# A routed mixture of experts inside a fused four-layer kernel: results stay in their slots and the next layer gathers and weighs them

## The chip, the cores and the metric

The kernel runs on one core of one Trainium2 chip. A core has a matmul engine (TensorE, PE), a vector engine (VectorE, DVE), an activation engine (ScalarE, ACT), a general-purpose engine (GpSimd, POOL) and a sync engine (SyncE, SP), each with its own instruction queue; they meet through semaphores. Two on-chip memories, SBUF and PSUM (where matmuls write), have 128 partitions; DRAM lies outside and is reached by DMA. POOL, SP and ACT can issue DMAs. An indirect DMA, issued by POOL, takes a list of row numbers, one per partition, and moves one row of DRAM for each: from SBUF to DRAM it scatters, the other way it gathers.

The metric is the time of one execution on the device in microseconds, as the median of several runs. The profile is of one execution of its own.

## The reference

Four layers follow one another on the same 8,192 tokens of 128 features in float32 (32 x 256 x 128 at the input, regrouped from layer to layer). Each layer is an attention-like block and a feed-forward block, with a residual addition and a normalization in front of each. Layer 0 has a state-space block and an expert-choice mixture of 16 experts. Layer 1 has a linear attention and the mixture below. Layer 2 has an attention with 16 heads of 8 features over sequences of 256 tokens and a low-rank mixture. Layer 3 has a smoothing block and a block of attention and a mixture with one expert per token.

What matters here is the feed-forward block of layer 1. Each token takes its two best of eight experts, weighed by a softmax over the two scores:

```
logits = xf @ gate_w + gate_b
top_w, top_i = jax.lax.top_k(logits, K)            # K = 2
gw = jax.nn.softmax(top_w, axis=-1)
combine = (gw[:, :, None] * one_hot(top_i, E)).sum(axis=1)
for e in range(E):                                  # E = 8
    h = gelu(xf @ w1[e] + b1[e])                    # 128 -> 512
    out = out + combine[:, e:e+1] * (h @ w2[e] + b2[e])
shared = gelu(xf @ ws1 + bs1) @ ws2 + bs2
return out + shared
```

The kernel computes only the two experts that a token has chosen.

## The kernel before

**Data.** The activations stay in SBUF for the whole kernel as `K.x`, 128 partitions x 64 blocks x 128 features; block j holds tokens 128j to 128j + 127. `NT` is 64, `P` and `D` are 128.

**Slots.** The class `Slots` holds the machinery of routing, once for layer 1 (`slots1`, tensors `f1_rows` and `f1_back`, two ranks: first and second choice) and once for layer 3 (`slots3`, `f3_rows` and `f3_back`, one rank). `rows` is a tensor in DRAM with one region of 8,448 rows per expert. A row has 130 floats (520 bytes): the token's 128 normalized features, the row of `back` to which its result belongs, and its weight. `back` holds first as many rows that nobody reads, for slots without a token, and behind them one row for each token and rank, in the order of the tokens.

**Fill.** `Slots.fill` runs in layer 0's feed-forward stage. It writes every slot of `rows` with zeros and with the slot's own number as its destination, so that an empty slot's result goes to a row that nobody reads. POOL makes the numbers (iota, L328) in one of two `blank` buffers and issues a DMA of 390 KB (L332), 88 for each of the two `Slots`.

**Sends.** In layer 1, while PE computes the shared expert (`rise` and `fall`, L1550 to L1574), coroutines advanced by `beside` normalize tokens, compute the gate and its best two, and count out a slot for each (`places`); DVE writes the slot numbers into two `slot` tiles from a pool of two buffers. Then POOL writes the destination (`belongs`, an iota, L368) and the weight (a copy, L1407) into the rows and issues, for each block and rank, one indirect DMA (`send`, L473): 128 in all, in four chunks of 16 blocks, the first rank and then the second.

**Experts.** `Slots.experts` goes through 72 groups of 256 slots (40 in layer 3). A group belongs to one expert; its first slot and its expert come from small tables and are read into registers. `fetch` loads the 256 rows (`xs`, on SP) and the weights, and PE transposes them; `rise` computes h (L533, L539); `fall` computes o (L549, L553), DVE multiplies by the weight column (`y`, L555), and POOL issues two scatters of 128 rows (`result`, L479). One step of the loop runs `rise` of one group, `fetch` of the next and `fall` of the one before.

**Entry of layer 2.** In `l2_attn` a generator `enter` works in groups of eight blocks. For each it loads `back`'s first and second rank (`results`, L574, 512 KB on SP, three buffers), adds each to `K.x` (DVE, L2022), takes the statistics of the blocks and finishes the normalization in small steps. `beside` advances it by two steps each time that the attention calls it; `rows` runs it further where the next two blocks aren't ready. POOL then makes the normalized blocks `xn` (L2039), which PE transposes (L1732) and projects (L1743). Between projection and scores the heads pass through DRAM (`d<-low`, `k<-d`, `q<-row`).

**Order.** In these stages the program's own order holds for PE, ACT and DVE, in the experts for SP too. A scheduler arranges POOL, and SP elsewhere. Each queue runs in order, so an instruction that waits holds those behind it. Writes to different rows of one DRAM tensor are declared free of each other (`free`).

## Time and profile before

| what | value |
|---|---|
| runs | 3314.72, 3316.81 (median), 3318.75 us |
| profiled execution | 3323.56 us; its span 3321.8 us |
| granted PE clock | 0.89 of full speed |
| PE busy | 2661.6 us (80%) |
| weight loads (PEld) busy | 1897.2 us (57%) |
| DVE busy | 1843.3 us (55%) |
| ACT busy | 1409.0 us (42%) |
| POOL busy | 844.5 us (25%) |
| POOL's DMAs (queue 0) | 97.92 MB, 7.7% of 16 engines' span |
| SP's and ACT's DMAs (queue 1) | 237.01 MB, 25.1% |

The stages stand one after another in the span:

| us | stage | PE busy | DVE busy | POOL busy | DMA share |
|---|---|---|---|---|---|
| 363-674 | layer 0's experts, with the fill | 255.21 of 311 | 138.06 | 123.74 | 0.60 |
| 674-859 | layer 0's experts, after the fill | 180.19 of 185 | 107.93 | 0.57 | 0.07 |
| 859-1026 | layer 1's attention and gate | 137.63 of 167 | 127.99 | 32.17 | 0.03 |
| 1026-1301 | layer 1's shared expert, routing and sends | 156.37 of 275 | 34.97 | 116.23 | 0.14 |
| 1310-1636 | layer 1's routed experts | 321.96 of 326 | 124.15 | 137.02 | 0.20 |
| 1636-1860 | layer 2's attention, with its entry | 167.32 of 224 | 157.73 | 28.58 | 0.52 |
| 1860-2240 | layer 2's attention | 341.20 of 380 | 266.19 | 30.55 | 0.43 |
| 2400-3104 | layer 3's attention, with its sends | 539.11 of 704 | 505.92 | 186.06 | 0.38 |
| 3104-3247 | layer 3's routed experts | 114.82 of 143 | 57.48 | 76.52 | 0.26 |

How to read it: the shares of the whole span are averages over stages with different limits, so a change is judged in its stage. A row of the groups gives line, engine, operation, written and read tiles, shape and count; then busy time and the mean of one in ns; then the engine's idle time just before these instructions and what ended it. The chain of waits goes back from the last instruction, at each step to what released it; a piece has its start, its length and its name. "issue" is time in which the engine waited for nothing that the profile shows, and "remote" or "another core or an unknown queue" stands where no instruction in the profile accounts for the release. A DMA on POOL is shown while POOL works on the issue; the transfer itself is apart.

### The profile page before, as it was taken

The numbers are of one execution on the slowest core, as the hardware profiler recorded it, in microseconds if no ns is written. First come the engines' busy times: TensorE is split into PE (matmuls) and PEld (weight loads), VectorE is DVE, ScalarE is ACT, GpSimd is POOL, SyncE is SP. The second block draws the span as 40 slices with busy tenths as digits, with TensorE's granted clock in tenths as the row PEclk, the third lists the DMA queues.
The fourth block names the chain that finished last, engine by engine and source line by source line (L and its number), as shares of the span: only waits on it lengthen the run. The fifth ranks groups of instructions, "written<-read, shape, count | busy, mean of one in ns | idle before, by whom it ended". The sixth has DMA issues, their size and how long they took to land.

```text
span 3321.8 us, 59216 instructions
## 1 busy us (share of the span) xinstructions
PE 2661.6 (80%) x21597; PEld 1897.2 (57%) x21598; DVE 1843.3 (55%) x5368; ACT 1409.0 (42%) x2988; POOL 844.5 (25%) x1227
## 2 busy tenths in 40 slices
PE   5999778999795457999778998988988888786580
PEld 4765444446564335888656777757655555554460
DVE  6115445436874111333368877755788877774446
ACT  3323432223463222333425555557246655553123
POOL 0001444300015341444310010001501332323463
PEclk9899889999898778999869999997979988997795
DMA  2377455620002010122165444420054444440223
GB/s 67 110 247 238 177 233 228 232 73 6 11 1 88 26 35 15 60 62 61 55 180 152 131 138 141 131 64 1 8 147 119 116 115 115 122 115 13 83 80 107
DMA packets 263262, 340.80 MB, mean 103 GB/s; under 512 B 34598, under 2 KB 231062, under 8 KB 254780
## 3 DMA queue, kind: packets, MB, share of 16 engines
q1 hardware_dynamic: 231228, 237.01, 25.1%
q0 software_dynamic: 27584, 97.92, 7.7%
q8 instruction: 171, 2.80, 0.4%
q10 hardware_dynamic: 4160, 2.10, 0.2%
q14 instruction: 119, 0.97, 0.1%
HBM read 156.72 MB, written 177.83 MB: 101 GB/s over the span
## 4 chain that ended last, share of the span: by engine, by line
PE 36%; DVE 16%; issue 5%; another core or an unknown queue 5%; ACT 4%; DMA 3%; POOL 2%; SPq 1%; DVEq 0%; POOLq 0%; ACTq 0%
DVE top L1803 6%; PE hp L533 5%; PE o L549 5%; PE t L1849 4%; PE o L1870 4%; PE s L1791 2%; DMA q<-row 2%; PE o L1568 2%; POOL f_back L479 1%; ACT e L1857 1%; DVE st_x L241 1%; PE hp L1554 1%; PE m L1743 1%; PE m L1908 1%
## 5 line engine op out<-in xcount | busy, mean ns | idle before, releaser
L1803 DVE TENSOR_REDUCE top<-s 128x3 f32<-128x384 f32 (+1 forms) x1024 | 598.6, 616 | 212.9 <-PE s L1702 111.2
L1857 ACT ACTIVATE e<-t 128x384 f32<-128x384 f32 (+1 forms) x1024 | 493.7, 546 | 140.0 <-PE s L1702 76.6
L1849 PE MATMUL t<-q,k 64*128 64x256 f32 (+1 forms) x2048 | 422.9, 313 | 103.0 <-ACT e L1857 77.9
L1791 PE MATMUL s<-k,q 48*128 48x256 f32 (+1 forms) x2048 | 446.5, 333 | 12.7 <-DVE top L1803 10.1
L1849 PEld LDWEIGHTS t<-q,k 64*128 64x128 f32 x2048 | 303.4, 195 | 185.4 <-ACT e L1857 108.9
L1791 PEld LDWEIGHTS s<-k,q 48*128 48x128 f32 x2048 | 312.9, 201 | 27.4 <-DVE top L1803 20.0
L479 POOL DMA_INDIRECT f_back<-y,place x224 | 216.3, 965 | 313.1 <-DVE y L555 171.8
L539 ACT ACTIVATE h<-hp,w 128x256 f32<-128x256 f32 x368 | 154.6, 471 | 328.6 <-PE hp L533 287.2
L1870 PE MATMUL o<-e,val 128*32 128x256 f32 (+1 forms) x4096 | 270.2, 385 | 0.0
L549 PE MATMUL o<-w,h 128*128 128x128 f32 x1472 | 214.3, 284 | 0.0
L533 PE MATMUL hp<-xT,w 128*128 128x256 f32 x736 | 195.2, 405 | 21.2 <-DVE xT L524 15.6
L549 PEld LDWEIGHTS o<-w,h 128*128 128x128 f32 x1472 | 183.5, 193 | 7.7
L2039 POOL TENSOR_SCALAR xn<-x_sb,mean_x,r_x 128x128 f32<-128x128 f32 x64 | 53.0, 836 | 441.7 <-PE m L1732 387.2
L1870 PEld LDWEIGHTS o<-e,val 128*32 128x32 f32 x4096 | 112.0, 114 | 91.9 <-issue 38.8
L533 PEld LDWEIGHTS hp<-xT,w 128*128 128x128 f32 x736 | 134.2, 195 | 46.2 <-DVE xT L524 20.2
L1554 PE MATMUL hp<-xnT,shared 128*128 128x512 f32 x128 | 74.2, 709 | 103.4 <-ACT h L1558 93.2
L1702 PE MATMUL s<-hideq,pick 64*128 64x128 bf16 x1024 | 151.5, 231 | 0.0
L473 POOL DMA_INDIRECT f_rows<-row,slot x128 | 122.9, 960 | 110.3 <-ACT h L1558 66.9
L1702 PE MATMUL t<-hidek,pick 64*128 64x128 bf16 x1024 | 146.2, 226 | 0.0
L555 DVE TENSOR_TENSOR y<-o,xs 128x256 f32<-128x256 f32 x112 | 47.4, 424 | 164.4 <-PE o L553 149.2
L766 PE MATMUL up<-wc,hT 128*128 128x128 f32 x768 | 129.2, 309 | 0.0
L1574 DVE TENSOR_TENSOR x_sb<-x_sb,o 128x512 f32<-128x512 f32 x16 | 11.0, 687 | 209.9 <-remote 98.9
(515 smaller groups left out, 5392.8 us busy)
## 6 DMA issues: line engine op xcount, KB each, us to landing
f_rows<-blank POOLq DMA_DIRECT2D x176, 390.0 KB
tz<-kpad SPq DMA_DIRECT2D x64, 512.0 KB
d<-high SPq DMA_DIRECT2D x128, 256.0 KB
d<-low SPq DMA_DIRECT2D x128, 256.0 KB
q<-d SPq DMA_DIRECT2D x128, 256.0 KB
k<-d SPq DMA_DIRECT2D x128, 256.0 KB
xs<-f_rows SPq DMA_DIRECT2D x112, 130.0 KB
t<-f_back SPq DMA_DIRECT2D x24, 512.0 KB
```

The source lines that it names most:

```text
L473: i = self.K.nc.gpsimd.indirect_dma_start(self.rows, bass.IndirectOffsetOnAxis(ap=slot, axis=0), row, None)
L479: i = self.K.nc.gpsimd.indirect_dma_start(self.back, bass.IndirectOffsetOnAxis(ap=place, axis=0), row, None)
L533: nc.tensor.matmul(hp[:, i, :], w[:, (c + i) * P : (c + i + 1) * P], xT, start=True, stop=True,)
L539: nc.scalar.activation(h[:, c + i, :], hp[:, i, :], act, bias=w[:, b1 : b1 + 1])
L549: nc.tensor.matmul(o[:, i, :], h[:, c, i * P : (i + 1) * P], w[:, F + c * D : F + c * D + D], start=c == 0, stop=False,)
L766: nc.tensor.matmul(o, hT[:, 2 * blk + b, s : s + P], wc[:, j, cs], start=j == 0, stop=False)
L1702: nc.tensor.matmul(t.rearrange("p (n q) -> p n q", n=3)[:, 0:3:2, 64 * n : 64 * n + 64], pick[r, n, :], hide[name][r], start=False, stop=n ...
L1791: nc.tensor.matmul(s[:, lo:hi], q[r, p, h * P : (h + 1) * P], k[r, p, 0 : hi - lo], start=h == 0, stop=not causal and h == 1,)
L1803: nc.vector.tensor_reduce(tops[b][:, :, j, p], out_of["s"][:, 0:used].rearrange("q (h k) -> q h k", h=3 if causal else 2), axis=AX.X, op=A ...
L1849: nc.tensor.matmul(t[:, kh * SEQ : kh * SEQ + SEQ - skip], k[r, p, kh * P : (kh + 1) * P], q[r, p, skip:SEQ], start=kh == 0, stop=not caus ...
L1857: nc.scalar.activation(e, t, AF.Exp)
L1870: nc.tensor.matmul(o[32 * i : 32 * i + 32, skip:SEQ], val[b % RING][:, kh, 4 * m + i, 16 * s : 16 * s + 32], e[:, kh * SEQ : kh * SEQ + SE ...
```

## The change

Only layer 1's routing and what lies around it changes; layer 3 keeps its rows of 130 floats and its scatters.

- **Rows.** `slots1` has rows of 128 floats (512 bytes): tokens alone. `belongs` and the weight copy are gone for layer 1. Slot numbers and weights are written into tiles that live until layer 2 has used them (`K.slot_of`, `K.weight_of`).
- **Results.** `y` is a plain copy of `o`, and a group's 256 results go back with one DMA on SP (`put`) into the same slots of `f1_back`. The place copy is gone for layer 1.
- **Token loads.** In both layers the load of a group's tokens is issued a step earlier in the loop: `tokens(g + 2)` at its head. In layer 1 the register with the slot's number is read once for the load and once for the store.
- **Entry of layer 2.** For each block and rank, POOL gathers the token's result from its slot (`get`, an indirect DMA into one of 24 buffers), and DVE multiplies it by the weight and adds it to `K.x` in one instruction (`scalar_tensor_tensor`). Statistics are taken by single blocks.
- **Fill.** `slots3` is filled as before. Both `f1_rows` and `f1_back` are now filled with zeros from one `blank` buffer, by 88 DMAs of 384 KB each, whose source is one row repeated six times in each partition.

```diff
@@ -305,18 +305,22 @@
 
 
 
-    GROUP, WIDE, NE = 256, D + 2, 8
+
+    GROUP, NE = 256, 8
     ROOM = NT * P + GROUP
 
-    def __init__(self, K, es, tag, ranks):
-        self.K, self.tag, self.ranks = K, tag, ranks
+    def __init__(self, K, es, tag, ranks, bring):
+        self.K, self.tag, self.ranks, self.bring = K, tag, ranks, bring
+        self.WIDE = D + 2 if bring else D
         self.groups = ranks * NT * P // self.GROUP + self.NE
         self.count = self.NE * self.ROOM
         dram = K.pool(es, tag + "slots", 1, DRAM)
         self.rows = dram.tile([self.count, self.WIDE], F32, name=f"{tag}_rows")
-        self.back = dram.tile([self.count + ranks * NT * P, D], F32, name=f"{tag}_back")
-
-    def fill(self, pool):
+        most = self.count + (ranks * NT * P if bring else 0)
+        self.back = dram.tile([most, D], F32, name=f"{tag}_back")
+
+    def fill(self, pool, other):
+
         nc = self.K.nc
         n = 6
         blank = [pool.tile([P, n, self.WIDE], F32, name=f"blank{i}") for i in range(2)]
@@ -330,6 +334,10 @@
                 allow_small_or_imprecise_dtypes=True,
             )
             nc.gpsimd.dma_start(rows[i], t)
+        for t in (other.rows, other.back):
+            rows = t.rearrange("(c p n) w -> c p n w", p=P, n=n)
+            for i in range(self.count // P // n):
+                nc.gpsimd.dma_start(rows[i], blank[0][:, 0:1, 0:D].to_broadcast([P, n, D]))
 
     def begin(self, pool, most):
 
@@ -463,6 +471,19 @@
         nc.vector.scalar_tensor_tensor(mine, mine, float(G), which, ALU.mult, ALU.add)
         nc.vector.tensor_scalar_min(start, mine, float(self.count - G))
 
+    def put(self, at, y):
+
+        i = self.K.nc.sync.dma_start(
+            self.back[bass.ds(at, self.GROUP)].rearrange("(n p) d -> p n d", p=P), y
+        )
+        self.free(self.tag + "put", i.ins)
+
+    def get(self, out, slot):
+
+        self.K.nc.gpsimd.indirect_dma_start(
+            out, None, self.back, bass.IndirectOffsetOnAxis(ap=slot, axis=0)
+        )
+
     def free(self, key, ins):
 
         self.K.tc.declare_no_dep(ins, group=key, reason="rows that differ")
@@ -497,17 +518,22 @@
             pt = K.pool(ps, tag + "gt", 2, PSUM)
             ph = K.pool(ps, tag + "gh", 4, PSUM)
             po = K.pool(ps, tag + "go", 2, PSUM)
-            state = {}
+            state, tokens_of = {}, {}
+
+            def where(g):
+                return nc.sync.value_load(
+                    start[0:1, g : g + 1], min_val=0, max_val=self.count - self.GROUP
+                )
+
+            def tokens(g):
+                xs = tokens_of[g] = gp.tile([P, N, self.WIDE], F32, name="xs")
+                nc.sync.dma_start(
+                    xs, self.rows[bass.ds(where(g), self.GROUP)].rearrange("(n p) w -> p n w", p=P)
+                )
 
             def fetch(g):
 
-                at = nc.sync.value_load(
-                    start[0:1, g : g + 1], min_val=0, max_val=self.count - self.GROUP
-                )
-                xs = gp.tile([P, N, self.WIDE], F32, name="xs")
-                nc.sync.dma_start(
-                    xs, self.rows[bass.ds(at, self.GROUP)].rearrange("(n p) w -> p n w", p=P)
-                )
+                xs = tokens_of.pop(g)
                 at = nc.vector.value_load(
                     expert[0:1, g : g + 1], min_val=0, max_val=(self.NE - 1) * LONG
                 )
@@ -515,8 +541,10 @@
                 nc.vector.tensor_copy(w, flat[:, bass.ds(at, REST)])
                 b2 = gp.tile([3, D], BF16, name="b2")
                 nc.vector.tensor_copy(b2, flat[0:3, REST:][:, bass.ds(at, D)])
-                place = gp.tile([P, N], mybir.dt.uint32, name="place")
-                nc.vector.tensor_copy(place, xs[:, :, D])
+                place = None
+                if self.bring:
+                    place = gp.tile([P, N], mybir.dt.uint32, name="place")
+                    nc.vector.tensor_copy(place, xs[:, :, D])
                 t = pt.tile([P, N * P], F32, name="t")
                 for i in range(N):
                     nc.tensor.transpose(t[:, i * P : (i + 1) * P], xs[:, i, 0:D], K.ident)
@@ -552,6 +580,10 @@
                         )
                     nc.tensor.matmul(o[:, i, :], self.every[0:3, :], b2, start=False, stop=True)
                 y = gp.tile([P, N, D], F32, name="y")
+                if not self.bring:
+                    nc.vector.tensor_copy(y, o)
+                    self.put(where(g), y)
+                    return
                 nc.vector.tensor_mul(y, o, xs[:, :, D + 1 : D + 2].to_broadcast([P, N, D]))
                 for i in range(N):
                     self.result(place[:, i : i + 1], y[:, i, :])
@@ -559,7 +591,10 @@
             with K.tc.manual_schedule(
                 engines={nc.tensor.engine, nc.scalar.engine, nc.vector.engine, nc.sync.engine}
             ):
+                tokens(0)
                 for g in range(-1, self.groups + 1):
+                    if g + 2 < self.groups:
+                        tokens(g + 2)
                     if 0 <= g < self.groups:
                         rise(g)
                     if g + 1 < self.groups:
@@ -950,8 +985,7 @@
             pos, pattern=[[1, SEQ]], base=0, channel_multiplier=0,
             allow_small_or_imprecise_dtypes=True,
         )
-        for slots in (K.slots1, K.slots3):
-            slots.fill(sp)
+        K.slots3.fill(sp, K.slots1)
         xs = sp.tile([P, 4, NB, 4, CAP], F32, name="xs")
         ew = K.pool(es, "f0e", 3)
 
@@ -1264,7 +1298,6 @@
         sp = K.pool(es, "l1", 1)
         xnT = sp.tile([P, NBLK, 512], F32, name="xnT")
         row = sp.tile([P, NT, S.WIDE], F32, name="row")
-        weight = sp.tile([P, NT], F32, name="weight")
         nmr = sp.tile([P, NT], F32, name="nmr")
         expert = sp.tile([1, S.groups], mybir.dt.int32, name="expert")
         start = sp.tile([1, S.groups], mybir.dt.int32, name="start")
@@ -1391,20 +1424,17 @@
             nc.vector.tensor_sub(e, tops[1], tops[0])
             nc.scalar.activation(e, e, AF.Exp)
             yield
-            slots = [lw.tile([P, n], mybir.dt.uint32, name=f"slot{i}") for i in range(2)]
+            slots = [t[:, lo:hi] for t in K.slot_of]
             yield from S.places(rw, lambda: hold.pop(lo), picks, slots)
             sum_e = new("sum_e")
             nc.vector.tensor_scalar_add(sum_e, e, 1.0)
             yield
-            w0 = row[:, lo:hi, D + 1]
+            w0, w1 = (t[:, lo:hi] for t in K.weight_of)
             nc.vector.reciprocal(w0, sum_e)
             yield
-            nc.vector.tensor_mul(weight[:, lo:hi], w0, e)
+            nc.vector.tensor_mul(w1, w0, e)
             yield
             for i in range(2):
-                S.belongs(row, lo, n, i)
-                if i == 1:
-                    nc.gpsimd.tensor_copy(w0, weight[:, lo:hi])
                 for j in range(lo, hi):
                     S.send(slots[i][:, j - lo : j - lo + 1], row[:, j, :])
             yield
@@ -2011,18 +2041,24 @@
 
 
         norm, after = K.norms
-        rp = K.pool(es, "a2r", 3)
+        rp = K.pool(es, "a2r", 24)
         closing = []
         ready = [0]
 
         def enter():
             for lo in range(0, NT, 8):
-                xb = K.x[:, lo : lo + 8, :]
-                for n in range(2):
-                    nc.vector.tensor_add(xb, xb, K.slots1.results(rp, n, lo))
-                    yield
-                for j in range(lo, lo + 8, 2):
-                    norm.take(K.x, j, j + 2)
+                got = {}
+                for j in range(lo, lo + 8):
+                    for n in range(2):
+                        got[j, n] = rp.tile([P, D], F32, name="t")
+                        K.slots1.get(got[j, n], K.slot_of[n][:, j : j + 1])
+                for j in range(lo, lo + 8):
+                    for n in range(2):
+                        nc.vector.scalar_tensor_tensor(
+                            K.x[:, j, :], got[j, n], K.weight_of[n][:, j : j + 1], K.x[:, j, :],
+                            ALU.mult, ALU.add,
+                        )
+                    norm.take(K.x, j, j + 1)
                     yield
                 for _ in norm.steps(lo, lo + 8):
                     yield
@@ -2621,10 +2657,17 @@
     with ExitStack() as es:
         K = Ctx(tc, ins, es)
         K.out = out
-        K.slots1 = Slots(K, es, "f1", 2)
-        K.slots3 = Slots(K, es, "f3", 1)
-        for stage in (l0_attn, l0_ffn, layer1, l2_attn):
+        K.slots1 = Slots(K, es, "f1", 2, False)
+        K.slots3 = Slots(K, es, "f3", 1, True)
+        for stage in (l0_attn, l0_ffn):
             stage(K)
+        with ExitStack() as two:
+
+            tp = K.pool(two, "two", 1)
+            K.slot_of = [tp.tile([P, NT], mybir.dt.uint32, name=f"slot_of{i}") for i in range(2)]
+            K.weight_of = [tp.tile([P, NT], F32, name=f"weight_of{i}") for i in range(2)]
+            layer1(K)
+            l2_attn(K)
         last = l3_ffn(K)
         middle(K, *next(last))
         for _ in last:
```

More of the change, by code (lines that the diff above doesn't have):

```diff
@@ L499, in experts, with fetch @@
             po = K.pool(ps, tag + "go", 2, PSUM)
-            state = {}
-            def fetch(g):
-                at = nc.sync.value_load(
+            state, tokens_of = {}, {}
+            def where(g):
+                return nc.sync.value_load(
                     start[0:1, g : g + 1], min_val=0, max_val=self.count - self.GROUP
                 )
-                xs = gp.tile([P, N, self.WIDE], F32, name="xs")
+            def tokens(g):
+                xs = tokens_of[g] = gp.tile([P, N, self.WIDE], F32, name="xs")
                 nc.sync.dma_start(
-                    xs, self.rows[bass.ds(at, self.GROUP)].rearrange("(n p) w -> p n w", p=P)
+                    xs, self.rows[bass.ds(where(g), self.GROUP)].rearrange("(n p) w -> p n w", p=P)
                 )
+            def fetch(g):
+                xs = tokens_of.pop(g)
                 at = nc.vector.value_load(
```

## The prediction

> **What bounds the kernel now.** I read the page first, then its chain of waits in the stretches that the change touches, then busy times per stretch, then groups of instructions.
>
> ```profile
> L479 POOL DMA_INDIRECT f_back<-y,place x224 | 216.3, 965 | 313.1 <-DVE y L555 171.8
> L2039 POOL TENSOR_SCALAR xn<-x_sb,mean_x,r_x 128x128 f32<-128x128 f32 x64 | 53.0, 836 | 441.7 <-PE m L1732 387.2
> L473 POOL DMA_INDIRECT f_rows<-row,slot x128 | 122.9, 960 | 110.3 <-ACT h L1558 66.9
> L1574 DVE TENSOR_TENSOR x_sb<-x_sb,o 128x512 f32<-128x512 f32 x16 | 11.0, 687 | 209.9 <-remote 98.9
> ```
>
> These four rows of the page concern us. An indirect DMA takes POOL about 0.96 us, and two starts in a series lie 1.26 us apart. The last row is odd: a DVE addition waits 98.9 us for something "remote" in a program of one core. The chain of waits for layer 1's routing (1010 to 1310 us) shows where:
>
> ```profile
> 1026.04 5.19 another core or an unknown queue
> 1031.28 7.17 another core or an unknown queue x2
> ...
> 1058.68 50.40 another core or an unknown queue
> ...
> 1155.52 19.92 another core or an unknown queue
> 1176.05 9.98 another core or an unknown queue
> ...
> 1219.42 17.52 another core or an unknown queue
> ...
> 1240.45 17.85 another core or an unknown queue
> ```
>
> That is 128 us of a stage of 275 us. The POOL sends to `f1_rows` run at 1014.8-1035, 1041-1103, 1144.8-1187 and 1212.7-1255, and each hole lies inside or at the end of such a series. Busy time over the second series:
>
> ```profile
> 1041.00:1063.00 22.00, 13.53 (x55) 8.60 (x54) 5.45 (x35) 8.83 (x15) 16.42 (x18) 0.70 0.48 144
> 1064.00:1087.00 23.00, 6.37 (x13) 2.65 (x12) 0.00 (x0) 0.00 (x0) 16.11 (x19) 0.58 0.15 49
> 1087.00:1109.00 22.00, 0.77 (x1) 0.00 (x0) 0.00 (x0) 0.00 (x0) 12.94 (x14) 0.50 0.13 42
> ```
>
> Columns: stretch, length, then busy time and count of PE, weight loads, DVE, ACT, POOL; clock, DMA share, GB/s. While POOL issues one indirect DMA after another, PE falls to 13 matmuls in 23 us and DVE and ACT to none; they wake at 1109.0, though PE's last matmul started at 1086.6. So PE's signals arrive late, with the DMA engines only 15% busy. I call this the freeze. Layer 3's series of 8 sends (10 us) show it too:
>
> ```profile
> 2780.37 5.95 another core or an unknown queue
> ...
> 2860.54 4.83 another core or an unknown queue
> ```
>
> From these: a series of n sends freezes about 1.26n - 5 us. The scatters of layer 1's experts, two per 4.44 us, show no such piece.
>
> The third place is the entry to layer 2:
>
> ```profile
> 1643.37 27.07 issue
> 1670.44 1.62 POOL xn L2039
> ```
>
> PE has nothing until the first normalized rows (`xn`) at 1670.4.
>
> **What the skill says.** The Trainium skill, "GPSIMD Engine Reference", section "When to use GPSIMD", says a pair of POOL's cores generates the descriptors of such a DMA, one the read and one the write side. "DMA: Bandwidth & Descriptors", section "Terms", puts those descriptors in rings in SBUF. Neither speaks of a freeze; if its cause is this generation, a gather must behave like a scatter. The same page's "Specifications" asks for 512 bytes per transfer for full rate; the 520-byte rows are above it, and the trace shows only a small gain to be had: packets of 4,160 B (eight rows) take 193 ns, those of 4,096 B 158 ns. "Perfetto Trace Analysis", section on SWDGE, says the shown end of such an instruction is the end of generation, not of the transfer; the trace agrees, packets follow it.
>
> **The change, part by part.** The sum is against the profiled execution, 3323.56 us (span 3321.8); the runs' median is 6.8 us lower, and I carry the difference over to it.
>
> *Sends (layer 1).* Still 128 at 1.26 us = 161 us. Gone are eight iotas, four weight copies and their waits: POOL waits 4.6 + 1.7 + 1.65 + 1.64 us between half-series plus about 0.8 us each, 13 us in all. DVE's slot casts lose their wait for a buffer. As the freeze ends with the series, most comes off the path: -10 (0 to -13).
>
> *Experts.* The stage 1310-1636 has PE busy 321.96 of 326 us. 144 scatters leave POOL, 72 stores of 128 KB go to SP behind `y`; the token loads stand two groups ahead of them in SP's queue. A 0.15 us copy per group leaves DVE (busy 124 of 326). PE's cover hides all: 0. Without it, the 72 copies would be worth 11 us.
>
> *Fill.* 176 DMAs of 390 KB become 88 of 390 KB and 176 of 384 KB, 104 MB in place of 70. Before:
>
> ```profile
> L332 POOL DMA_DIRECT2D f_rows<-blank x176 | 98.1, 557 | 54.4 <-POOL blank L328 51.5 <-issue 3.0
> ```
>
> The new ones have 768 pieces of 512 B each. Price of that: not shown; POOL's 16-piece DMAs at the start take 490-535 ns and the 128-piece ones 557, so about 0.56 ns a piece and an estimate of 0.93 us for 768; at worst proportional, 3.3 us. At the 226 GB/s of before the fill lasts 461 us, 363.6 to 825; the first send is at 1014.8 and POOL does nothing between 674 and 859. Hidden: 0. At 3.3 us it ends near 990, POOL's constants for layer 1 (at 859 now) come that late, and it costs about 130.
>
> *Entry of layer 2.* Out go 16 loads of 512 KB (on SP, the second one behind the fills of q and k until 1659.4) and 16 additions of 1.217 us (19.5 us). In come 128 gathers of 128 rows, priced by the sends: 161 us on POOL, and 128 weigh-and-add instructions on DVE; the like form at L1518 takes 343 ns alone, about 0.28 in a row: 36 us. DVE gains 17 us, in a stretch (1636-1860) where it is busy 158 of 224: 3 on the path (0 to 17). In the order that the changed program is built in, POOL has 32 gathers ahead of the first `xn`. The last store lands about 1644 (the last expert output at 1639, the store of 128 KB some 3 us, a guess between 2 and 5); 32 x 1.26 = 40, so `xn` comes at 1684.5, not 1670.4: +14 (5 to 20).
>
> *Freeze by the gathers.* The other 96 come in series of 2, 8, 14, 14, 2, 16, 8, 8, 16 and 8, with two `xn` between (0.8 us each). By the rule: 0, 5, 12.6, 12.6, 0, 15, 5, 5, 15, 5 = 75 us, in an attention with PE at 90% and a signal between engines at every step, so it is exposed. But 24 buffers pace them: DVE frees two per 2 us, and a frozen DVE frees none, which breaks a series off. I take 55; bounds 0 (gathers don't freeze) and 96 x 1.26 = 121 (no gap at all helps).
>
> Sum: -10 + 0 + 0 + 3 + 14 + 55 = +62; 3316.8 + 62 = 3379.
>
> **Rivals.** *Gathers don't freeze.* Nothing in the trace is a gather; the freeze may belong to writes into DRAM. Then -10 + 3 + 14 = +7, 3324, and with xn on time and the copies gained -14, 3303. *The freeze is due to rows of 520 bytes* and falls away with 512: then 128 us come off layer 1's stage, which is bounded by its 161 us of sends instead: they end at about 1190, the stage near 1200 in place of 1301: -100, plus 3 at the entry: about 3215. This ends on the other side; it decides if series of 512-byte rows run without late signals. Against it: layer 3's scatters into `f3_back` have 512-byte rows, and after four to six in a row (3144.6-3152.3) a transpose that ended at 3150.7 woke DVE at 3153.3, 2.6 us late. *The fill freezes or blocks layer 0's experts.* POOL would be busy generating about half the time, up to 825. Before, at 0.56 of 1.77 us, nothing froze. If PE loses a tenth of 460 us: +46 on the sum, about 3425; if generation is proportional, 3510. *Nothing moves* would need gathers hidden entirely and no gain, part of the first rival.
>
> **How the numbers follow.** Freezing gathers 0.44 (all slower; own range 3340 to 3430). Gathers without freeze 0.30 (3300 to 3340: faster 0.17, same 0.06, slower 0.07). No freeze at all 0.14 (faster). Fill 0.12 (slower). Faster 0.31, same 0.06, slower 0.63; 0.2% is 6.6 us, about what a measurement can tell from no change. Range 3225 to 3455: it takes in the first two cases, the milder third of the no-freeze case and the milder fill; outside are about 0.10 below and 0.08 above.
>
> **What would show it.** Right: in the chain of waits of 1690-1900, pieces of "another core or an unknown queue" of 5 to 15 us beside runs of gathers, some 40 to 70 us in sum; the first `xn` about 14 us later after the last expert matmul than the 32 us of before; the routing stage shorter by about 10 us with its holes still there; experts at 4.44 us a group. Wrong: holes gone from the routing stage (512-byte rows), gathers with PE at its old pace, or layer 0's experts ending later than 859. My forecast falls first if the freeze belongs to DRAM writes.

## The result, and the profile after

The changed kernel took 3410.08 us (median of 4 runs, 3409.13 to 3415.03), the kernel before 3316.04 (3314.72 to 3318.75): a ratio of 1.0285, 95% interval 1.0268 to 1.0301, so 94 us slower. The forecast was 3379, in a range of 3225 to 3455, with 0.63 for slower. The profiled execution's span went from 3321.8 to 3413.3 us, 91.5 more.

One thing has to be known for all that follows: the freeze beside series of sends was there in the measurement above and in experiments 9 to 12 (kernel before at 3316 to 3324 us), and absent in experiments 1 to 8 (3137 to 3147 us), on one chip in both ways at different times; every ratio is to the kernel before in the same group of runs.

In the profiles without the freeze no engine waits for "remote" anywhere. Stage times are of single profiles, and the same code varies in them: layer 2's attention of the kernel before took 555.2 and 558.1 us in two profiles without the freeze, and 559.5 and 565.4 in two with it. A difference under some 6 us in that stage says nothing.

The lost time by stage, from the start and end of the same PE instructions in both profiles:

| up to | before, us | after, us | shift | added here |
|---|---|---|---|---|
| last `o` of layer 0's experts | 861.3 | 862.9 | +1.6 | +1.6 |
| last `o` of layer 1's shared expert | 1301.6 | 1311.2 | +9.6 | +8.0 |
| end of layer 1's experts (the last product that prepares layer 2's weights) | 1643.4 | 1653.0 | +9.6 | 0 |
| first transposition of `xn` in layer 2 | 1672.1 | 1693.9 | +21.8 | +12.2 |
| last output projection of layer 2 | 2231.6 | 2325.5 | +93.9 | +72.1 |
| end of the span | 3321.8 | 3413.3 | +91.5 | -2.4 |

From the page of the changed kernel, the groups of sends, gathers, normalized rows (`xn`), and the addition of the shared expert:

```profile
L494 POOL DMA_INDIRECT f_rows<-row,slot_of x128 | 122.9, 960 | 120.8 <-ACT h L1588 67.0
L483 POOL DMA_INDIRECT t<-f_back,slot_of x128 | 122.9, 960 | 82.0 <-DVE x_sb L2057 36.2
L2075 POOL TENSOR_SCALAR xn<-x_sb,mean_x,r_x 128x128 f32<-128x128 f32 x64 | 50.6, 797 | 335.5 <-PE m L1762 320.4
L1604 DVE TENSOR_TENSOR x_sb<-x_sb,o 128x512 f32<-128x512 f32 x16 | 11.0, 687 | 191.6 <-PE o L1598 92.0
```

A gather costs POOL exactly what a send does, 960 ns, as the prediction had priced it. The last row no longer names "remote" first, but the holes in the routing stage are still there, now with rows of 512 bytes. Two stretches of it, in the columns that the prediction explains:

```profile
1087.00:1109.00 22.00, 0.00 (x0) 0.00 (x0) 0.69 (x1) 4.41 (x12) 16.70 (x18) 0.57 0.16 53
1226.00:1260.00 34.00, 3.99 (x19) 2.21 (x17) 0.69 (x1) 0.00 (x0) 22.98 (x24) 0.61 0.14 48
```

The changed kernel's chain of waits in layer 2's first 300 us has the start as one piece, and then holes that were not there before:

```profile
1652.97 40.96 issue
...
1725.97 3.65 another core or an unknown queue
1730.36 3.47 another core or an unknown queue
...
1799.80 3.67 another core or an unknown queue
...
1838.63 5.21 another core or an unknown queue
...
1888.62 5.11 another core or an unknown queue
...
1922.03 8.05 another core or an unknown queue
```

The longer series of gathers ran at 1653-1693 (32), 1700-1710 (8), 1714-1731 (14), 1750-1765 (12), 1789-1812 (16), 1833-1855 (16), 1877-1892 (12) and 1918-1928 (8): each hole lies in or behind such a series, and the attention stops losing time against the kernel before after about 1980. All eight such holes up to 1990 make 33 us, in pieces of 1.7 to 8 us; the prediction had looked for 40 to 70 us in pieces of 5 to 15. The waits in 1693 to 1960 say who was kept waiting:

```profile
DVE top L1833 <- remote: 41.6, 11, 5.2
ACT e L1887 <- remote: 32.9, 7, 6.6
```

The columns are the total in us, the number of waits and the longest. Both engines wait for PE's products of scores, and both for a release that no instruction accounts for. The kernel before has no such row there.

Busy time over the part of layer 2's attention with the same 2154 matmuls, before and then after:

```profile
1672.00:1881.00 209.00, 181.41 (x2154) 137.16 (x2154) 164.02 (x531) 94.13 (x221) 24.75 (x30) 0.84 0.55 156
```

```profile
1694.00:1980.00 286.00, 213.06 (x2154) 155.22 (x2154) 187.63 (x619) 94.41 (x221) 115.57 (x125) 0.71 0.41 116
```

DVE has 23.6 us more work. The matmuls themselves take 32 us more, at a granted clock of 0.71 in place of 0.84: PE is made to wait and had a lower clock as well.

### The profile page after: what moved, and what is told of

It reads as the page before. It is cut to its first block, busy times and chain, and to the rows that moved or that the text cites. A ratio compares the mean times of both kernels' runs of the same rounds, so it can differ in the third digit from the quotient of the medians.

```text
span 3413.3 us, 59764 instructions
## 1 busy us (share of the span) xinstructions
PE 2701.8 (79%) x21598; PEld 1922.6 (56%) x21598; DVE 1866.6 (55%) x5408; ACT 1409.2 (41%) x2988; POOL 902.7 (26%) x1197
## 3 DMA queue, kind: packets, MB, share of 16 engines
q0 software_dynamic: 39744, 130.80, 12.2%
## 4 chain that ended last, share of the span: by engine, by line
PE 36%; DVE 16%; issue 8%; another core or an unknown queue 4%; ACT 3%; POOL 3%; DMA 2%; SPq 1%; DVEq 0%; POOLq 0%; ACTq 0%
DVE top L1833 7%; PE hp L561 4%; PE o L577 4%; PE t L1879 4%; PE o L1900 4%; POOL f_back L500 2%; PE s L1821 2%; PE o L1598 2%; PE hp L1584 1%; ACT e L1887 1%; DVE st_x L241 1%; PE m L1773 1%; DMA q<-row 1%; PE m L1938 1%
## 5 line engine op out<-in xcount | busy, mean ns | idle before, releaser
L1900 PE MATMUL o<-e,val 128*32 128x256 f32 (+1 forms) x4096 | 278.0, 390 | 3.2 <-issue 3.0
L494 POOL DMA_INDIRECT f_rows<-row,slot_of x128 | 122.9, 960 | 120.8 <-ACT h L1588 67.0
L483 POOL DMA_INDIRECT t<-f_back,slot_of x128 | 122.9, 960 | 82.0 <-DVE x_sb L2057 36.2
L801 PEld LDWEIGHTS up<-wc,hT 128*128 128x128 f32 x768 | 109.2, 214 | 10.3 <-issue 2.8
```

The costliest lines, as they stand in the source:

```text
L483: self.K.nc.gpsimd.indirect_dma_start(out, None, self.back, bass.IndirectOffsetOnAxis(ap=slot, axis=0))
L494: i = self.K.nc.gpsimd.indirect_dma_start(self.rows, bass.IndirectOffsetOnAxis(ap=slot, axis=0), row, None)
L801: nc.tensor.matmul(o, hT[:, 2 * blk + b, s : s + P], wc[:, j, cs], start=j == 0, stop=False)
L1900: nc.tensor.matmul(o[32 * i : 32 * i + 32, skip:SEQ], val[b % RING][:, kh, 4 * m + i, 16 * s : 16 * s + 32], e[:, kh * SEQ : kh * SEQ + SE ...
```

## The experiments

**1 and 2. Without gathers.** The changed kernel with plain loads in place of the gathers, on SP and on POOL.

```diff
-                        K.slots1.get(got[j, n], K.slot_of[n][:, j : j + 1])
+                        K.slots1.get(got[j, n], 2 * j + n)
...
-        self.K.nc.gpsimd.indirect_dma_start(
-            out, None, self.back, bass.IndirectOffsetOnAxis(ap=slot, axis=0)
-        )
+        self.K.nc.sync.dma_start(out, self.back[slot * P : (slot + 1) * P, :])   # 1; gpsimd in 2
```

> The changed kernel with each of the 128 gathers at layer 2's entry replaced by a plain load of 128 consecutive rows of the same tensor, issued by SP; it leaves out the choice of rows by slot, so layer 2 adds the wrong rows. Same bytes, buffers and DVE work, nothing on POOL but xn. Theory (a dense series of indirect DMAs on POOL delays PE's signals): the 72 us that layer 2's attention lost go, and so does most of the 12 us of its start: 3325 to 3345, no pieces of 'another core or an unknown queue' between 1690 and 1960. Rival (the loss is the extra work and waits of the entry itself, on DVE and in the buffers): it stays above 3385.

> As the run before, but the plain loads of 128 rows stay on POOL, 128 of them in the same places of its queue; again layer 2 adds the wrong rows. Theory (indirect DMAs): POOL's plain DMA of 128 pieces takes 0.56 us, the attention keeps its pace, 3325 to 3350. Rival (any dense series of DMAs from POOL freezes PE): the pieces of 'unknown queue' stay beside the series, some 20 to 50 us of them, 3360 to 3410.

Measured: 3167.63 us, ratio 1.0107 (1.0079 to 1.0136), and 3166.0 us, 1.0092 (1.0062 to 1.0121), the kernel before at 3137.01. The times expected had been meant for a machine with the freeze, and there was none: no engine in either profile waits for "remote". So neither run could tell the freeze from its rivals. As ratios the expected times were 1.003 to 1.009 for the first, which is just missed, and 1.003 to 1.010 for the second, which is met. What the runs do show is that some 30 us are lost with neither gathers nor freeze.

**5 and 6. The two kernels again, unchanged.**

> The kernel before, unchanged, for a profile of it beside the others of this group: in the first four experiments the kernel before ran in 3137 us, 179 less than in the prediction's measurement, and their profiles show no holes beside the sends. Theory A (the freeze is a property of the chip in use or of its state): where the routing stage takes some 160 us, the holes are gone; where it takes 275, they are there, and in both the ratio to the kernel before is 1. Theory B (the profiled kernels e1 to e4 differ in the order of the stage): holes here in any case.

> The changed kernel, unchanged, on the same chip as the run before. Where the freeze is there: 1.028 of the kernel before, as measured. Where it is not: if all of the 72 us lost in layer 2's attention were freeze, what is left is the start (12 us) and the routing stage at its gain (-10), so 0.998 to 1.006; if the entry itself costs (POOL's queue ahead of xn, buffers, DVE's work), 1.015 to 1.03.

Measured: 3140.6 us, ratio 0.9993 (0.9976 to 1.0009), and 3188.99 us, ratio 1.0133 (1.009 to 1.0177). The kernel before in the stretches that the prediction showed, this time:

```profile
1064.00:1087.00 23.00, 17.88 (x91) 12.14 (x90) 7.40 (x28) 8.64 (x12) 16.36 (x19) 0.85 0.15 50
1087.00:1109.00 22.00, 21.86 (x127) 15.24 (x125) 4.95 (x14) 7.95 (x11) 16.51 (x19) 1.00 0.16 53
```

POOL is as busy with its sends (19 instructions in each stretch; 19 and 14 with the freeze) and the DMA share is the same, but PE has 91 and 127 matmuls instead of 13 and 1. From its first `hp` to its last `o` the stage took 156.0 us; with the freeze it took 275.2. The freeze is worth 119 us there, and it does not come from the program alone: theory A held, in the form that something changes with time on one chip (experiments 5 to 8 and 11 and 12 ran on the same one).

Without the freeze the changed kernel loses 1.33%, not 2.85. Its attention, from the first transposition to the last output projection, took 588.5 us against 555.2: +33.3. In experiments 1 and 2 it took 579.5 and 583.5. So of the 33 us, 24 to 28 are there without any gather, and gathers add 5 to 9, which is hardly more than the same code varies by. With the freeze the loss was 72, so some 39 are the freeze's.

**9. DVE's part alone.** The 24 us equal DVE's extra work. So the kernel before got DVE's part of the new entry, with its large loads kept.

```diff
+        one = K.pool(es, "a2one", 1).tile([P, 1], F32, name="one")
+        nc.vector.memset(one, 1.0)
...
-                for n in range(2):
-                    nc.vector.tensor_add(xb, xb, K.slots1.results(rp, n, lo))
-                    yield
-                for j in range(lo, lo + 8, 2):
-                    norm.take(K.x, j, j + 2)
-                    yield
+                got = [K.slots1.results(rp, n, lo) for n in range(2)]
+                for j in range(lo, lo + 8):
+                    for n in range(2):
+                        nc.vector.scalar_tensor_tensor(
+                            K.x[:, j, :], got[n][:, j - lo, :], one[:, 0:1], K.x[:, j, :],
+                            ALU.mult, ALU.add,
+                        )
+                    norm.take(K.x, j, j + 1)
+                    yield
```

> The kernel before with DVE's part of the new entry alone: its 512 KB loads stay, but the 16 additions over eight blocks become 128 multiply-adds of one block (weight one), and statistics are taken by single blocks. If DVE is on the path of layer 2's attention, as the 25 us suggest that are lost there with plain loads too: 20 to 28 us slower (1.006 to 1.009). If the attention hides it, as the prediction had it: at most 5 us.

Measured: 3342.07 us, ratio 1.0071 (1.0046 to 1.0097), the kernel before at 3315.59. The attention took 584.0 us against the 559.5 of the kernel before with the freeze: +24.5, and DVE's busy time rose from 1843.3 to 1867.2 us: +23.9. So the path lengthened by as much as DVE's work, and no cover is seen. Three instructions in a row of DVE's timeline in this run:

```profile
1690.13 1.01 DVE L1803 TENSOR_REDUCE top<-s 128x3 f32<-128x384 f32 x2
1691.05 0.73 DVE L2025 SCALAR_TENSOR_TENSOR x_sb<-t,one,x_sb 128x128 f32<-128x128 f32 x2
1691.81 0.29 DVE L241 BATCH_NORM_STATS2 st_x<-x_sb 128x6 f32<-128x128 f32 x1
```

The maxima (`top`), which PE's next product waits for, stand in the same queue between these; a maximum that is next in the queue starts 0.73 us later for each such pair. (128 such additions also make other steps of the entry and another rhythm of the calls; that these cost nothing was not tried by itself.)

**11. Plain loads on POOL, with the freeze.** The kernel of experiment 2, unchanged.

> The second experiment again (plain loads of 128 rows on POOL in place of the gathers, so layer 2 adds the wrong rows), for a chip on which the freeze is there. If only indirect DMAs freeze PE: from the first projection on, the attention ends some 29 us later than in the kernel before, as where there is no freeze, instead of 77, and no holes of unknown cause beside the series. If any DMA issued by POOL in series does: 60 us or more. On a chip without the freeze: 1.009 again.

Measured: 3343.14 us, ratio 1.0079 (1.005 to 1.0107), the kernel before at 3324.12; this time the freeze was there, with the routing stage's holes at their places. Between 1640 and 2010 the chain has no piece of unknown cause and no engine waits for "remote", and the attention took 584.4 us, +24.9 over the kernel before (with plain loads and no freeze it was +28.3 in experiment 2). With gathers and the freeze it was +72.1. So it is indirect DMAs that freeze PE, and gathers do it like scatters; plain DMAs of 128 pieces, in the same queue and number, don't. They start only 0.53 us apart, so a series of them is shorter than one of gathers; but length alone is not it either, since the changed kernel's own fill, 264 plain DMAs from POOL between 367 and 736 us, 1.4 us apart on average, in the execution with the freeze, has no wait for "remote" beside it.

**8 and 12. Sends with a rest.** The kernel before, with something else for POOL to do after each send, and POOL in program order in layer 1 (the second change stands twice, for both loops of the shared expert).

```diff
+        rest = sp.tile([P, 900], F32, name="rest")
...
                 for j in range(lo, hi):
                     S.send(slots[i][:, j - lo : j - lo + 1], row[:, j, :])
+                    nc.gpsimd.memset(rest, 0.0)          # 128 x 900 floats
...
-                engines={nc.tensor.engine, nc.scalar.engine, nc.vector.engine}
+                engines={nc.tensor.engine, nc.scalar.engine, nc.vector.engine, nc.gpsimd.engine}
```

> The kernel before with a POOL memset of some 0.9 us after each of the 128 sends, and POOL in the program's order in layer 1, so that sends start about 2.2 us apart. Where the freeze is there: if the rate of indirect DMAs makes it, the holes shrink to under 30 of 128 us and the stage is bounded by its sends, 282 us from 1015: 1297, about as long as before (0.99 to 1.005); if POOL's being busy makes it, the holes grow with the series and the stage ends 80 to 120 us later. Where it is not: the stage is bounded by the sends, 282 in place of 161 us, 1.02 to 1.04.

> The eighth experiment again (a POOL memset of 0.9 us after each send, sends 2.2 us apart), for a chip on which the freeze is there. If the rate of indirect DMAs makes it: the routing stage is bounded by the sends alone and ends near 1300 to 1310, holes under 30 us in sum, total within 0.5% of the kernel before. If POOL's being busy makes it: holes longer than before's 128 us, the stage ends near 1400, 1.02 to 1.04. On a chip without the freeze: 1.027 again.

Measured: without the freeze 3229.42 us, ratio 1.027 (1.0226 to 1.0313), as expected of a stage bounded by its sends. With the freeze 3285.63 us, ratio 0.99 (0.986 to 0.994): faster than the kernel before, and the one variant that beat both kernels; "within 0.5%" had been too careful. The stretches in which the kernel before, with the freeze, showed 13 matmuls and 1:

```profile
1064.00:1087.00 23.00, 17.88 (x85) 11.66 (x85) 9.68 (x29) 9.24 (x13) 21.12 (x25) 0.85 0.10 32
1087.00:1109.00 22.00, 22.00 (x140) 16.66 (x139) 4.49 (x13) 7.95 (x11) 20.17 (x23) 1.00 0.11 35
```

POOL is busier than ever, and PE works. No engine waits for "remote" between 1020 and 1290; the stage took 174.4 us from first `hp` to last `o` instead of 275.2. That the freeze was there in this very execution is seen in layer 3, whose sends have no rests:

```profile
DVE top L1805 <- remote: 21.9, 4, 6.2
ACT xT L1736 <- remote: 21.3, 4, 5.9
```

The kernel before has 22.0 and 21.6 us in these two rows. So POOL's being busy is not the cause, and sends spaced in this way do not freeze PE. Two things were changed at once, though: the memset alone, the program order alone, and a pause without an instruction in it were not tried. In the chain of waits it is now the last send, and the load of tokens behind it, that lets the experts start:

```profile
1276.05 2.32 DMA f_rows<-row,slot
1278.56 2.25 DMA xs<-f_rows
```

The first transposition of tokens is at 1280.9, against 1313.0 in the kernel before; the sends started from 1017.4 to 1276.0, some 2.04 us apart. Where the freeze is absent it is no remedy but costs 2.7%.

**3. Rows of 520 bytes again.** The changed kernel with two columns of zeros behind each token.

```diff
-        self.WIDE = D + 2 if bring else D
+        self.WIDE = D + 2
...
+        nc.gpsimd.memset(row[:, :, D:], 0.0)
...
-                nc.gpsimd.dma_start(rows[i], blank[0][:, 0:1, 0:D].to_broadcast([P, n, D]))
+                w = rows.shape[3]
+                nc.gpsimd.dma_start(rows[i], blank[0][:, 0:1, 0:w].to_broadcast([P, n, w]))
```

> The changed kernel with 520-byte rows in layer 1's slots again (two columns of zeros behind the token), everything else as changed. Theory: row size does not matter to the freeze: 3400 to 3420, holes in the routing stage as in the changed kernel. Rival (the 520-byte rows cause the late signals, and 512-byte rows have shortened the holes in the routing stage from 128 to 73 us): slower by 20 to 60 us, 3430 to 3470.

Measured: 3216.29 us, ratio 1.0269 (1.0239 to 1.0298), against 1.0133 for the changed kernel without the freeze (experiment 6). The routing stage is as short as in the others (1058.5 to 1216.6), so there the row's size costs nothing; the loss is in the fill, whose last DMA starts at 817.4 instead of 735.3 and with which layer 0's experts end at 889.1 instead of 862.0 (experiment 6; 864.2 in experiments 1 and 4). As a test of the freeze it is void, since there was none; against the rival speak the changed kernel's own sends of 512 bytes, which froze PE in the first measurement (the two stretches shown there).

**4 and 7. Fewer buffers, and pacing.** The changed kernel with eight buffers for gathered rows; in 4, also POOL in program order in layer 2, one entry step per call and gathers issued two blocks ahead. Only the buffers are shown.

```diff
-        rp = K.pool(es, "a2r", 24)
+        rp = K.pool(es, "a2r", 8)
```

> The changed kernel with its gathers paced: eight buffers in place of 24, POOL in the order of the program in layer 2, one step of the entry per call in place of two, and a block's two gathers issued two blocks ahead of their use, so that about one gather falls on 2 us and the entry lasts as long as the attention needs; 16 gathers stand ahead of the first xn in place of 32. Theory: few holes left in the attention and a start 10 to 15 us earlier: 3325 to 3360. Rival (the extra work itself costs the time): above 3385.

> The changed kernel with eight buffers for gathered rows in place of 24, nothing else. A gather then waits for an addition four blocks back. If long series are what costs: 10 to 40 us faster than the changed kernel. If the place of the gathers ahead of xn in POOL's queue is what costs: the same or slower by up to 30, since POOL then waits at a gather with xn behind it.

Measured: 3190.89 us, ratio 1.0183 (1.0156 to 1.0209), and 3182.36 us, 1.0117 (1.0074 to 1.0159). The start became shorter, as expected: from the last weight product to the first transposition 26.9 us (16 gathers ahead of `xn`) and 31.0 (24 ahead) instead of 41.0 (32 ahead). But the attention took 593.1 and 592.5 us, not less than the 588.5 with 24 buffers; the 4 us between them are no more than the same code varies by. Without a freeze there was nothing for pacing to save. Whether pacing removes the freeze of the gathers, as the rests do for the sends, was not seen.

**10. Weighing on ACT.** The changed kernel with gathers into three buffers of eight blocks, ACT for the multiplication and 16 large additions on DVE; shown in part.

```diff
+                        nc.scalar.activation(
+                            got[n][:, j, :], got[n][:, j, :], AF.Identity,
+                            scale=K.weight_of[n][:, lo + j : lo + j + 1],
+                        )
...
+                    nc.vector.tensor_add(xb, xb, got[n])
```

> The changed kernel with the weighing moved: gathers land in buffers of eight blocks, ACT multiplies each block by its weight, and DVE adds eight blocks at once, 16 additions as in the kernel before. 38 gathers instead of 32 stand ahead of the first xn. If DVE's extra work is what the attention loses besides the freeze: from the first projection to the end of the attention 15 to 25 us less than the changed kernel, the first xn 5 to 8 us later, in all 8 to 20 us faster than it. If any extra work at the entry costs the same, whichever engine has it: no gain, or slower by up to 25.

Measured: 3421.45 us, ratio 1.0326 (1.0292 to 1.0359), with the freeze. DVE's busy time fell to 1841.1 us (1866.6 in the changed kernel), but the attention took 640.1 us, 8.5 more than in the changed kernel. There is no gain, the outcome that the expectation gave for extra work costing the same on whichever engine does it. Its chain has the holes of the gathers, one of 8.00 us among them, and buffers of eight blocks let POOL issue 38 gathers before the first `xn`; ACT has 128 more instructions and 34.6 us more work (1443.8 us, 1409.2 in the changed kernel). Which of these ate DVE's 24 us is open. So the parts need not add: what DVE's work costs alone (experiment 9) is not what one gets back by taking it off DVE beside frozen gathers.

## Why the prediction was right, and where its sizes were off

The sign held, and so did the mechanism that the prediction gave the most weight; the sum was 62 and the profile shows 91.5. Part of that is luck: the freeze could as well have been absent from the measurement. The change would then have been slower too, by 42 us, but mostly by a term that the prediction had put at 3.

- **Freeze by the gathers: 55 predicted, 39 measured**, plus 5 to 9 for gathers without a freeze, within the bounds of 0 and 121. That a gather freezes like a scatter, the step with the most doubt, is shown by experiment 11 against the changed kernel. The prediction had rested it on what the Trainium skill says ("GPSIMD Engine Reference", "When to use GPSIMD"), that a pair of POOL's cores generates the descriptors of a DMA issued there, one the read side and the other the write side. The runs agree with the conclusion. But by that section plain DMAs issued on POOL come from the same pair, and in experiment 11 they don't freeze PE, so generation as such is not the cause; what is, stays open.
- **Entry, DVE's part: 3 predicted, 24 measured.** This is the step that failed most. I took cover from DVE's share, 158 us busy of 224, and gave 3 of 17 us to the path. In experiment 9 all of it is on the path. The page of the kernel before had hinted at it, in the lines of its longest chain:

```profile
DVE top L1803 6%; PE hp L533 5%; PE o L549 5%; PE t L1849 4%; PE o L1870 4%; PE s L1791 2%; DMA q<-row 2%; PE o L1568 2%; POOL f_back L479 1%; ACT e L1857 1%; DVE st_x L241 1%; PE hp L1554 1%; PE m L1743 1%; PE m L1908 1%
```

  DVE's maxima stand first, so what joins their queue can delay them. The count was short, too: a weighing took 0.35 us, not 0.28, so 128 of them made 44.6 us in place of 36, and 25 more than the 19.6 of the additions that left.
- **Sends: -10 predicted, +8 measured.** From first `hp` to last `o` the old routing took 275.2 and 269.9 us in two profiles with the freeze, the new one 279.2, 278.9 and 278.9 in three, and it begins later as well. The step took the stage to get shorter by the gaps removed between sends. But POOL waits for the slots of the next sends, and the gaps saved became such a wait:

```profile
1069.45 0.95 POOL L494 DMA_INDIRECT f_rows<-row,slot_of  x1 [12.85 <-DVE slot_of L434]
```

  The 33rd send starts at 1069.4 (1061.6 before), the 65th at 1144.7 (1144.8) and the last at 1255.2 (1254.0). Without the freeze the sends do end 12 us earlier (the last starts at 1177.0, before at 1189.0), and the stage is no shorter for it: 157.7 us, before 156.0. So there the sends are not what bounds it. That it began later is seen in POOL's timeline. The last multiplication of layer 1's attention (`q`) had stood behind four sends and stands behind seven now, since sends no longer wait for the iotas:

```profile
1018.79 0.96 POOL L473 DMA_INDIRECT f_rows<-row,slot  x1 [0.30 <-issue]
1019.77 1.27 POOL L1480 TENSOR_TENSOR q<-q,qr 128x512 f32<-128x512 f32 x1
```

```profile
1022.86 0.96 POOL L494 DMA_INDIRECT f_rows<-row,slot_of  x1 [0.30 <-issue]
1023.85 1.27 POOL L1510 TENSOR_TENSOR q<-q,qr 128x512 f32<-128x512 f32 x1
```

  PE waited 4.1 us for it, and 1.8 before. The first shared matmul is 5.7 us later with the freeze and 7.3 without (1027.6, 1034.9); in the latter, transpositions after the wait start 0.21 us apart where 0.11 was usual, with a granted clock of 0.54 from 1027.6 to 1034.9, which was 1.00 in the kernel before. I had counted what POOL loses, not who stands in its queue. Whether a gap in the series also gives PE time to recover was not tried.
- **Start: +14 predicted, +12.2 measured**, 12.5 without the freeze, and with 16 or 24 gathers ahead of `xn` it shrinks as the step says (experiments 4 and 7).
- **Experts: 0 and 0.** From the first transposition of tokens to the last product that prepares layer 2's weights it took 330.4 us before and 330.3 after.
- **Fill: 0 predicted, +1.6 measured,** no more than that stage's end varies by in profiles of the same code (859.9 to 866.3). The DMAs of 768 pieces took POOL 0.79 to 0.81 us as medians, close to the estimate of 0.93 and far from the proportional 3.3, and the fill ended at 736, earlier than the 825 estimated, as the transfers ran at 292 GB/s.
- **The rivals.** "Gathers don't freeze" is what happens where nothing freezes, but it would have ended at +42 (1.0133), not +7, for DVE's sake. Its lower end, -14, does not come out of its terms either: without the start and with the copies gained they make -10 + 3 - 11 = -18. "Rows of 520 bytes" is refuted by the 512-byte sends that froze; its sum of about 3215 also left out the start's 14 us without a reason. The fill rival did not occur; with 520-byte pieces layer 0's experts did end later, by 25 to 27 us in experiment 3.

In sum: 24 for DVE and the other 48 of the attention's 72 for gathers (5 to 9 of them without a freeze), 12 for the start, 8 for the sends, 1.6 for the fill, -2.4 at the end. The split of the 72 is worked out from different runs, and experiment 10 warns that the two parts need not be independent.

## What to carry to other kernels

An instruction that joins the queue of an engine on the chain of waits can cost its full length, however idle that engine looks on average; here 128 small weighings in place of 16 large additions, next to the maxima that the chain runs through, cost all of their 24 us. Long series of indirect DMAs from POOL are a risk: at one time they held up PE for more than a hundred microseconds, at another not at all, and a change has to be judged in both. Plain DMAs in the same places avoided it (experiment 11, which leaves out the choice of rows); spacing the sends gained 1% with the freeze and cost 2.7% without. Removing a wait from a queue lets what stood behind it pass; ask which instruction it now stands in front of.

## What the runs showed of the hardware

- Indirect DMAs issued by POOL 1.26 us apart kept PE's signals back for up to 50 us at a time in some groups of runs, and not in others with the same program on the same chip: 3316 to 3324 us against 3137 to 3147 for the kernel before. Its routing stage took 275 or 156 us. What differs between these times was not found in the profiles.
- 2.04 us apart, with a memset between, they did not, though POOL was busy 21 of 23 us and layer 3's sends in the same execution did. Plain DMAs of 128 pieces, 0.53 us apart, did not either.
- A gather of 128 rows of 512 bytes and a scatter of the same take POOL 0.96 us alike; a plain DMA of 768 pieces took 0.79 to 0.81 (medians), of 128 pieces 0.55 to 0.56.
- In experiment 3 the 88 fills of `f1_rows` with pieces of 520 bytes came 2.4 us apart (602.6 to 814.7); in the changed kernel those of `f1_back` with pieces of 512 bytes came 1.5 us apart (606.4 to 735.3).
- After a wait of 3.9 us in experiment 6, PE's transpositions started 0.21 us apart instead of 0.11, at a granted clock of 0.54 for the 7 us that were looked at; after one of 1.8 us in experiment 5 the clock stayed at 1.00.
